# A static plan for four graph attention layers on 32 graphs: priorities re-stated, with an addition for each eighth of the work of the first three and the last three graphs

## Chip, cores and metric

The kernel runs on one core of one Trainium2 chip. The metric is the time of one execution on the device in microseconds (us); lower is better. An execution of this kernel lasts about 3440 us.

## What is computed

The input is a batch of 32 graphs (`x`, 32 x 512 nodes x 256 features, float32) and one adjacency matrix for all of them (`adj`, 512 x 512 integers). Each graph goes, independently of the others, through four residual layers. Cut to what matters:

```python
def gat(h, mask, W, a, slope):           # one graph attention head
    v = h @ W
    e = leaky_relu(v @ a_src [:, None] + v @ a_dst [None, :], slope)
    return softmax(where(mask, e, -big), axis=-1) @ v

for layer in (L0, L1, L2, L3):
    h = relu(layernorm(x))
    x = x + layer(h)
# L0: 4 heads of 64 columns, masked, elu
# L1: relu(h @ W1 + b1), a full (unmasked) attention over 512 columns + residual,
#     relu(. @ W2 + b2), a masked attention over 256 columns + residual, relu
# L2: masked attention (own node always in), elu
# L3: masked attention, relu
```

All matrix products are in float32 and run on TensorE (PE). Per graph these are the projections, the four 512 x 512 attention matrices times the values of L0, the full attention of L1, and the three masked attentions of L1, L2 and L3, besides the transposes.

## The kernel before

**Recording, then planning.** The kernel does not issue instructions as its loops run. It records *pieces*: `do(engine, ns, outs, ins, run)` (`Plan.add`) notes one piece of work with an estimated duration, its engine and the tiles that it writes and reads, and works out which pieces it must follow. A graph is recorded by `plan.begin()` and 535 pieces (the set-up has 97). The list `plan.graphs` holds 33 entries: entry 0 is the set-up (loading of weights, masks and their transposes), entries 1 to 32 are the 32 graphs.

**The order.** `Plan.order()` then plays the whole program through on a small event model: five engines (PE; VectorE, here DVE; ScalarE, ACT; GpSimd, POOL; and the DMA queue of SyncE, SP), a fixed delay from a piece to its followers (`LAG`, `SAME`, `MORE`), a port that POOL shares with those DVE pieces that read no PSUM, and a stock of buffers (`SLOTS`). Up to `DEPTH` = 5 graphs are in work at once. Whenever an engine is free, the ready piece with the lowest key is taken, where

```python
            urgency = URGENCY if b else FIRST
            ...
                p.key = (max(0, b - 1) * PERIOD - urgency[n], b, n)
```

`b` is the graph, `n` the place of the piece in its recording, and `PERIOD` = 103600 ns. So one table, `URGENCY`, holds a number of nanoseconds for each piece of a graph and serves all 32 graphs alike; a second table, `FIRST`, serves the set-up. The order that comes out fixes the order of the instructions on every engine: each instruction is tied to the one before it on its engine. Nothing is reordered at run time, an engine that has to wait holds all that stands behind it, and only semaphores decide when something starts.

**Fillers.** Where the plan sees PE without work for 400 ns or more, it puts transposes of a constant into a spare PSUM tile, `filled` (L1017), behind the piece that comes before the gap:

```python
FILL, FILL_NS, FILL_FROM = 0.6, 110, 400
...
                    before.fill = int(FILL * gap / FILL_NS) if gap >= FILL_FROM else 0
```

They compute nothing that is used. Their number tells how long a gap the plan saw: one filler for each 110 / 0.6 = 183 ns of it.

**Names that matter below.** Every graph runs the same chains:

- Layer norm: `stats`, `mv` (DVE), `rstd` (POOL, L598 and L599), `shift` (DVE, L605), `h` (ACT, L613), then transposes `tr<-h` on PE (L398) and copies into `hT`.
- A masked attention (`gat`, and `gat_heads` for L0): projection `mm<-w..,hT` (L408), scores spread over the partitions `row<-v` or `row<-st` (PE), row maxima `left`, `peak` (DVE, L654), columns `ca`, `cb` (DVE, L677, L678), a transpose `tr<-cb` (PE, L632), `turned` (ACT), a write and a broadcast read through DRAM (`line`, `rb`, L636 and L644), then four times `y` (DVE, L697), an addition on POOL (L707 or L715) and an exponential on ACT (`pt`, L708 or L722), and the product `mm<-v,pt` or `mmh<-vh,pt` (PE, L408).
- The full attention of L1: `mm<-wfc,out1T`, a maximum over all nodes that goes over PE (`row<-tmax`, L398), a few small DVE operations on `c`, one exponential on ACT (`c<-c`, L859), the transpose `tr<-c` (PE, L632), `ra` (ACT, L870), `ptf` (DVE, L877), the products `mm<-hfc,ptf`.

`transposes` and `product` record a PE piece as several matmuls. In the trace a 257-column float32 matmul of the program stands as two records, and a transpose as one.

Of the kernel before, what the change touches and what calls it, by code (L numbers as in the profile page):

```python
# [36 lines left out]
PERIOD = 103600  # L37
# [4 lines left out]


URGENCY = [
    49957, 66495, 153342, 82735, 144893, 18248, 163947, 104419, 59651, 169283, 167420, 27958, 91780, 230242,
    195004, 201919, 109150, 118275, 41409, 148351, 105924, 84158, 33663, 128315, -31046, 92771, 80073,
    -45028, 28235, 136777, -16929, 40188, 120535, 69018, 81157, 34057, 45864, 64938, 93847, 22979, 32782,
    -10095, -7685, 78515, -28222, 19420, -8026, 14562, 65514, 92596, 50809, 54059, 90452, -2420, 84889,
    -14583, 182093, 91531, 6874, 128004, -23771, -69759, 210945, 103417, 96629, 177264, 97081, 141216,
    228810, 79944, 208774, 181698, 34991, 127254, 226356, -9989, 145084, 102532, 51302, 57785, 135746,  # L50
    80518, 8900, 128919, 64999, 72213, 100118, -191301, 129287, 126778, 107678, 38434, 214310, -59056,
    21096, 128569, -77796, 31871, 74871, 45424, 52264, -8376, 19505, -47500, 133347, 67984, 70285, 186177,
    -15984, 104650, 146444, -6977, 74654, 209924, -4928, 74371, 174294, 40423, 51951, 50262, 29464, 45416,
    3988, 20540, -30268, 143961, 32626, 29520, 89804, -46895, -71848, 192873, -94019, -16097, 82357,
    -169645, 44440, 58074, 23239, 29426, 38323, 69931, 62358, 28167, 54402, 35577, -76917, -57030, -27704,
    46576, -51547, -24313, -49157, 37623, -166471, -262408, -40277, -75897, 2495, -34811, -74370, 10822,
    -15615, -38619, -14324, 87924, -14732, 53506, -26615, -76490, 65133, 111389, 71959, 93636, 216417,
    118024, 163785, 26618, -73110, 16741, 9419, -10974, -26368, 86308, 35587, -14529, 9505, -23652, 31209,
    -35827, 87676, 57894, 76693, 67541, -81967, -32754, 78132, 16981, 15839, 11266, -39752, -44185, -180983,
    -106465, -45466, -89834, -11687, 103426, 151973, 157389, 186709, 237443, 270307, 278957, 17921, 218966,  # L60
    105429, 178416, 116249, 84788, 142806, 50637, 86803, 147442, 126624, 122625, -24526, 224818, 181273,
    122134, 261099, 188560, 278444, 309233, 202098, 46668, 146708, 13559, -27972, -149859, 4547, -115510,
    38885, 107791, -163000, 38869, -279727, -120416, -64868, -65585, -103808, 25837, -296121, 16410, -66665,
    -247882, -82470, -195328, -56781, -67125, -74463, -260380, -10356, -293322, -28794, -66573, -118165,
    117861, -244495, 33153, -14981, 71927, -75326, 49632, -75897, 12372, -59742, -253914, -34455, -280537,
    60459, -56427, -20405, -76842, -84804, -76638, -87008, 6362, -96566, -92921, -140211, -40235, 9737,
    1430, 138501, -8164, -11585, -790, 92727, -18209, -59964, 33770, 120062, 48291, -69971, -116178, -43376,
    -75934, -22587, -855, -7366, 64764, -21815, -173536, -191622, -247, -89468, -141561, -5472, -71333,
    -71091, -23345, -35224, -60425, -31184, -36678, -96715, -93204, -104153, 122741, -103991, -49069,
    -52273, 103915, -129888, -87436, -90017, -84147, -248017, -153179, -142134, -195377, -246140, -94749,  # L70
    -281312, -209508, -156148, -170174, -173938, -110763, -202784, -90958, -123778, -230905, -217447,
    -158358, -191908, -181567, -150880, -166302, -173285, -145335, -192412, -213127, -112164, -79463,
    -80154, -45304, -115344, -213688, -61711, -71844, -179488, -7519, -10195, -123581, -92377, -130342,
    -156089, -168165, -158280, -78069, -97410, 20095, 52768, -118896, -100859, -22248, -140758, -98924,
    -171258, -214761, -144742, -191503, -188885, -161622, -179163, -210494, -197100, -75155, -143396,
    -114654, -120868, -88478, -67661, -85469, -105261, -231208, -147545, -195786, -143928, -132751, -203479,
    -51238, -198637, -307380, -218655, -234274, -292902, -81910, -227932, -110271, -9939, -267811, -133305,
    96531, -164689, -28167, 25068, -163586, -170683, -125323, -118603, -47000, -182274, -161878, -209482,
    -210149, -168999, -138546, -191158, -233690, -133535, -231298, -285256, -155744, -125493, -243944,
    -223209, -190911, -249846, -244877, -146750, -260327, -392277, -245282, -212678, -202761, -168108,  # L80
    -206988, -163184, -234077, -225292, -151778, -418885, -146975, -166246, -197351, -165479, -253278,
    -164022, -7427, -227404, -223194, -205947, -290945, -299944, -191474, -275233, -246375, -249699,
    -253455, -249835, -216585, -256193, -283065, -390887, -270743, -284915, -267017, -418553, -281245,
    -293102, -238408, -177593, -347600, -366149, -358476, -414408, -536943, -384769, -405112, -314429,
    -370595, -265928, -543033, -409858, -416969, -320333, -443009, -407966, -431291, -243310, -493060,
    -378266, -346645, -225670, -370270, -376164, -325328, -399421, -374586, -398079, -417234, -461239,
    -465521, -400816, -409787, -543463, -345783, -366473, -257474, -479888, -496847, -470513,
]
FIRST = [
    -31437, 25750, -1105, 144955, 89002, 275880, 128415, 204208, 154195, 226450, 96820, 179479, 7870,  # L90
    -118045, 26290, 146438, 138609, 157057, 205913, -16123, 59630, 57501, -56814, 5247, -4577, -6068,
    -45189, -27458, 74268, 87671, 62434, 55789, -15727, -51036, -133151, -170623, -122434, -106956, -88821,
    -45241, -84685, -17322, -151531, 663, -157813, -74980, -174232, -62374, -58576, 11927, -19486, -48352,
    77279, -175495, -146175, -169316, -241074, -142701, -178875, -141702, -62487, -96044, -41405, -94885,
    -228054, -41409, -191710, -235324, -125187, -188700, -74514, -165891, -142656, -170202, 6399, -96844,
    -155386, -142053, -171779, -291299, -271981, -405298, -401521, -247815, -210715, -198935, -245058,
    -90055, -125151, -183656, -54990, -77623, -143327, -261274, -244716, -325695, -246171,
]


# [43 lines left out]
class Plan:  # L144
# [57 lines left out]
    def order(self):  # L202


        for b, pieces in enumerate(self.graphs):
            urgency = URGENCY if b else FIRST
            for n, p in enumerate(pieces):
                p.waits = len(p.after)
                p.key = (max(0, b - 1) * PERIOD - urgency[n], b, n)
        free = {k: n for k, (n, _) in SLOTS.items()}  # L210
        held = [dict.fromkeys(SLOTS, 0) for _ in self.graphs]
        undone = [len(g) for g in self.graphs]
# [3 lines left out]
        events, n, oldest, admitted, done = [], 0, 0, 0, []  # L216
# [29 lines left out]
        while True:  # L246
            for e in range(len(LAG)):
# [3 lines left out]
                while ready[e]:  # L251
                    key, p = heapq.heappop(ready[e])
# [26 lines left out]
            while events and events[0][0] == now:  # L279
                _, kind, _, e, p = heapq.heappop(events)  # L280
# [789 lines left out]
```

## Time and profile before

| | |
|---|---|
| median of 3 runs | 3440.47 us (3440.38 to 3443.44) |
| the profiled execution's own time | 3439.76 us |
| its span, from first to last instruction | 3437.8 us |
| PE busy | 3397.8 us (99%), 18801 matmul records |
| DVE, ACT, POOL busy | 2629.5 us (76%), 1962.7 us (57%), 1657.1 us (48%) |
| mean granted TensorE clock | 0.998 |
| fillers (L1017) | 497, 59.5 us of PE's busy time |

Busy time counts an engine as busy while an instruction of its own is in work. A group of the profile is named by its source line, its engine, and output<-input tiles; "idle before" is the time that the engine stood still just ahead of the group's instructions. Where a row of the trace says `PEclk`, it is the share of the full TensorE clock that was granted in that stretch.

### The profile page before, as it was taken

Reading aid. Unit: us, or ns where it says so; the run is one execution under the profiler, and the core shown is the slowest. Engines: PE = TensorE matmul, PEld = TensorE weight load, DVE = VectorE, ACT = ScalarE, POOL = GpSimd, SP = SyncE. Lnnn points to the kernel's source line nnn. Section 1 sums busy time; section 2 is a strip of 40 time slices with the busy share of each in tenths; the row PEclk is TensorE's granted clock in tenths of the full one; section 3 lists DMA queues with packets and bytes.
Section 4 is the critical chain, followed back from the end, with each engine's and each line's share of the span. In section 5 each row is a group of like instructions: output and inputs, shape, how many; then the busy total and the mean of one; then the engine's idle time right before and its main releaser. Section 6 shows DMA issues by size and latency. Waiting matters only on the chain. (4 is left out here: it accounts for less than half of the span.)

```text
span 3437.8 us, 55266 instructions
## 1 busy us (share of the span) xinstructions
PE 3397.8 (99%) x18801; PEld 2861.4 (83%) x18801; DVE 2629.5 (76%) x8200; ACT 1962.7 (57%) x4109; POOL 1657.1 (48%) x2089
## 2 busy tenths in 40 slices
PE   7999999999999999999999999999999999999998
PEld 7788888888888888888888888888888888888887
DVE  8587877777777777777777877777878777777764
ACT  4555565565655565555566655556655655655543
POOL 3253554454544454545444545544544545544544
PEclk9999999999999999999999999999999999999999
DMA  3000110011110011110010110010110011110000
GB/s 111 19 29 14 35 38 31 17 38 32 35 38 26 22 38 32 35 38 26 22 38 29 37 38 26 22 37 29 38 38 21 27 32 35 38 32 16 32 19 28
DMA packets 77978, 110.51 MB, mean 32 GB/s; under 512 B 7169, under 2 KB 43521, under 8 KB 77697
## 3 DMA queue, kind: packets, MB, share of 16 engines
q1 hardware_dynamic: 77696, 106.98, 9.9%
q8 instruction: 150, 2.46, 0.3%
q14 instruction: 132, 1.07, 0.1%
HBM read 89.66 MB, written 17.30 MB: 31 GB/s over the span
## 5 line engine op out<-in xcount | busy, mean ns | idle before, releaser
L715 POOL TENSOR_TENSOR y<-y,farT_some 128x512 f32<-128x512 f32 x512 | 584.9, 1176 | 311.1 <-DVE y L697 308.3
L408 PE MATMUL mm<-v,pt 128*128 128x257 f32 x3072 | 704.1, 380 | 7.0 <-ACT pt L708 4.2
L697 DVE SCALAR_TENSOR_TENSOR y<-row,cc,rb 128x512 f32<-128x512 f32 x896 | 625.2, 742 | 73.1 <-DMA rb<-line 53.5
L408 PEld LDWEIGHTS mm<-v,pt 128*128 128x128 f32 x3072 | 575.5, 190 | 88.4 <-ACT pt L708 5.4
L722 ACT ACTIVATE pt<-y,ct 128x512 f32<-128x512 f32 x640 | 459.3, 719 | 291.2 <-POOL y L715 271.5
L408 PEld LDWEIGHTS mmh<-vh,pt 128*128 128x128 f32 x4096 | 483.3, 192 | 10.0 <-ACT pt L722 1.8
L408 PE MATMUL mmh<-vh,pt 128*128 128x65 f32 x4096 | 481.8, 272 | 1.4 <-DVE y L697 0.6
L408 PE MATMUL mm<-hfc,ptf 128*128 128x257 f32 (+1 forms) x2048 | 465.6, 381 | 0.5 <-DVE ptf L877 0.4
L408 PE MATMUL mm<-wfc,out1T 128*128 128x257 f32 x2048 | 464.4, 379 | 0.0
L408 PEld LDWEIGHTS mm<-wfc,out1T 128*128 128x128 f32 x2048 | 382.2, 189 | 53.6
L408 PEld LDWEIGHTS mm<-hfc,ptf 128*128 128x128 f32 x2048 | 380.8, 189 | 52.7 <-issue 2.0
L654 DVE CUSTOM_DVE_ANT_0 left<-row,far_nz 128x512 bf16<-128x512 f32 x640 | 413.9, 681 | 9.1 <-PE row L398 9.1
L707 POOL TENSOR_TENSOR y<-y,g 128x512 f32<-128x512 f32 x256 | 323.1, 1274 | 93.7 <-issue 42.9
L613 ACT ACTIVATE h<-xt,shift,rstd 128x256 f32<-128x256 f32 x512 | 277.5, 592 | 32.1 <-DVE shift L605 32.0
L598 POOL TENSOR_SCALAR rstd<-mv 128x4 f32<-128x4 f32 x128 | 34.3, 268 | 533.9 <-DVE mv L1014 356.0
L939 ACT ACTIVATE ez<-mm,rden 128x256 f32<-128x256 f32 x256 | 120.8, 472 | 238.6 <-DVE rden L1014 167.1
L408 PE MATMUL mm<-hT,w 128*128 128x512 f32 x512 | 233.2, 592 | 0.0
L654 DVE CUSTOM_DVE_ANT_0 left<-row,far_pos 128x512 bf16<-128x512 f32 x256 | 165.5, 685 | 86.5 <-PE row L398 86.5
L408 PE MATMUL mm<-out1T,wm 128*128 128x512 f32 x512 | 224.9, 592 | 0.0
L708 ACT ACTIVATE pt<-y 128x512 f32<-128x512 f32 x256 | 160.6, 628 | 82.7 <-POOL y L707 82.7
L1014 DVE BATCH_NORM_STATS2 stats<-xt 128x6 f32<-128x256 f32 x512 | 196.9, 414 | 5.6 <-DMA xt<-in_x_dram 5.2
L971 POOL TENSOR_TENSOR xt<-xt,rz 128x256 f32<-128x256 f32 x128 | 100.8, 797 | 199.7 <-ACT rz L970 196.3
(150 smaller groups left out, 5636.8 us busy)
## 6 DMA issues: line engine op xcount, KB each, us to landing
rb<-line SPq DMA_DIRECT2D x256, 256.0 KB
xt<-in_x_dram SPq DMA_DIRECT2D x32, 512.0 KB
out_dram<-xt SPq DMA_DIRECT2D x32, 512.0 KB
line<-turned SPq DMA_DIRECT2D x128, 2.0 KB
adj_sb<-in_adj_dram SPq DMA_DIRECT2D x1, 1024.0 KB
wfc<-in_L_gnn_W_fc_dram SPq DMA_DIRECT2D x2, 512.0 KB
a_row<-in_L_gnn_a_dram SPq DMA_DIRECT2D x3, 256.0 KB
a_row<-in_L_gnn_a_fc_dram SPq DMA_DIRECT2D x1, 512.0 KB
```

Source lines behind the costliest of these rows:

```text
L408: nc.tensor.matmul(o, lhsT=parts[k], rhs=parts[nk + k], start=(k == 0), stop=(k == nk - 1))
L598: do(POOL, 200, [rstd.all], [mv[:, :, 1]], lambda o, a: nc.gpsimd.tensor_scalar(o, a, EPS, None, ALU.add))
L613: lambda o, a, m, s: nc.scalar.activation(o, a, AF.Relu, bias=m, scale=s),
L654: return nc.vector.tensor_tensor_reduce(out=junk, in0=a, in1=far, scale=1.0, scalar=LOWEST, op0=ALU.add, op1=ALU.max, accum_out=o,)
L697: lambda o, a, c, b: nc.vector.scalar_tensor_tensor(o, a, c, b, ALU.add, ALU.max),
L707: do(POOL, 1255, [y.all], [y.all, g.all], lambda o, y, g: nc.gpsimd.tensor_tensor(o, y, g, ALU.add))
L708: do(ACT, 521, [pt[:, jt, :]], [y.all], lambda o, a: nc.scalar.activation(o, a, AF.Exp))
L715: lambda o, y, far: nc.gpsimd.tensor_tensor(o, y, far, ALU.add),
L722: lambda o, a, c: nc.scalar.activation(o, a, AF.Exp, bias=c),
L939: do(ACT, ns, [o.all], [z, scale], lambda o, a, s=scale, f=f: nc.scalar.activation(o, a, f, scale=s))
L971: do(POOL, 685, [xi], [xi, r.all], lambda o, a, b: nc.gpsimd.tensor_tensor(o, a, b, ALU.add))
L1014: made = p.run(*(r.ap() if isinstance(r, Ref) else r for r in p.args))
```

## The change

The tables of the plan change, and the key in `Plan.order()`; no operation, tile, buffer or constant of the model does. All numbers of `URGENCY` and `FIRST` are replaced. Two tables are new: `EARLY` for the first three graphs and `LAST` for the last three, each with three rows of eight numbers. A piece's place in the recording decides which of the eight it gets, and the number is added to its urgency. (`LAST`'s first row goes to the last graph, its second to the one before, and so on.)

```diff
 URGENCY = [
-    49957, 66495, 153342, 82735, 144893, 18248, 163947, 104419, 59651, 169283, 167420, 27958, 91780, 230242,
...
+    43943, 23247, 115444, 28195, 131913, 11021, 150223, 75332, 64495, 133886, 120583, -1101, 94222, 220028,
...
 FIRST = [
-    -31437, 25750, -1105, 144955, 89002, 275880, 128415, 204208, 154195, 226450, 96820, 179479, 7870,
...
+    -36661, 19893, -21726, 135503, 85633, 237464, 129132, 171706, 120477, 219412, 125455, 134502, -84836,
...
+EARLY = [
+    [127714, 124300, 140109, 1275316, 20684, 3710, 30790, 20023],
+    [21381, 1446513, 75479, -3218, 89835, 61799, 992, -5994],
+    [16582, -743, 947951, -35616, 537487, -26713, 362315, 602],
+]
+LAST = [
+    [136435, 122850, 411901, 1447410, 146100, 513359, -692128, 374735],
+    [14763, 42474, 104030, 510068, 166538, -178446, 1731034, 221293],
+    [5870, -6330, 13392, 2190, 30176, 62234, 471784, -1052314],
+]
...
+        more = {len(self.graphs) - 1 - k: row for k, row in enumerate(LAST)} | {1 + k: row for k, row in enumerate(EARLY)}
         for b, pieces in enumerate(self.graphs):
             urgency = URGENCY if b else FIRST
             for n, p in enumerate(pieces):
                 p.waits = len(p.after)
-                p.key = (max(0, b - 1) * PERIOD - urgency[n], b, n)
+                add = more[b][n * len(more[b]) // len(pieces)] if b in more else 0
+                p.key = (max(0, b - 1) * PERIOD - urgency[n] - add, b, n)
```

Below the tables the changed file's lines stand lower by 12, and below the new line of `Plan.order()` by 14 (L408 is then L422, L1017 is L1031).

## The prediction

> **What bounds the kernel now.** I read the page's busy times first, then the groups of PE with shapes kept apart, then PE's waits, then the stretches of the span, and last the order of time at the places that these point to.
>
> ```profile
> span 3437.8 us, 55266 instructions
> PE 3397.8 (99%) x18801; PEld 2861.4 (83%) x18801; DVE 2629.5 (76%) x8200; ACT 1962.7 (57%) x4109; POOL 1657.1 (48%) x2089
> L408 PE MATMUL mm<-v,pt 128*128 128x257 f32 x3072 | 704.1, 380 | 7.0 <-ACT pt L708 4.2 <-ACT pt L722 2.8
> L1017 PE MATMUL filled<-ident 128*128 128x128 f32 x497 | 59.5, 273 | 0.0
> ```
>
> PE is busy for all but 40.0 us of the span, and 59.5 us of the busy time is fillers. So PE's own work is 3397.8 - 59.5 = 3338.3 us, and 99.5 us (40.0 idle, 59.5 fillers) is all that any order could win. Is the work itself at PE's pace? In the order of time, 32 records of `mm<-v,pt` last 7.11 us where nothing disturbs them: taking off the last one's drain, 217 ns from start to start, in the middle and in the tail alike. That pace doesn't depend on the order.
>
> The Trainium skill (Perfetto Trace Analysis, Identifying the Most-Contended Engine) says that matmul busy time is a bad measure of headroom and that the busy share of LDWEIGHTS should be used instead. Here that is 83%, which would leave 17% of the span, an estimate of some 580 us, to a better order; the even 217 ns speak against it, and I go by the row.
>
> Where do the 99.5 us lie? First the fillers alone, then everything, by stretches (start and length, then busy us and instructions):
>
> ```profile
> 0.00:50.00 50.00, 12.85 (x108) 12.32 (x108) 0.93 0.57 190
> 50.00:100.00 50.00, 10.23 (x87) 9.39 (x84) 0.97 0.06 22
> 3300.00:3350.00 50.00, 8.02 (x66) 7.45 (x66) 1.00 0.05 17
> 3350.00:3400.00 50.00, 14.03 (x118) 13.16 (x118) 0.97 0.07 22
> 3400.00:3440.00 40.00, 13.26 (x114) 12.66 (x114) 0.93 0.10 34
> ```
>
> The reader sees fillers at both ends and (these rows hold 58.4 of the 59.5 us) next to none between. Of the middle, PE's rows are:
>
> ```profile
> 200.00:400.00 200.00, 199.00 (x1106) 1.00 0.08 26
> 400.00:600.00 200.00, 199.73 (x1072) 1.00 0.09 27
> 600.00:3000.00 2400.00, 2398.95 (x13180) 1.00 0.10 32
> 3000.00:3200.00 200.00, 200.00 (x1104) 1.00 0.10 30
> ```
>
> PE stands still for 2.3 us in these 3000. The middle can hardly get better; the ends can.
>
> **How the order moves.** Both programs hold the same 11136 PE instructions of the program besides fillers. The fillers are 497 before and 381 after. By place: start 194 -> 217 (the two long groups, 68 and 61, become 74 and 62, and 15 new ones come about 250 to 300 us in); end 303 -> 164. At the end the groups 27, 12, 23, 66, 77 become many groups of 2 to 15 and, last, 22 and 48: the chains of the last graphs, which ran one behind the other with nothing beside them, now lie beside each other, and the very last product is for two graphs (32 records by 2) rather than one.
>
> **What a filler stands for.** A filler is not the gap; the gap is filler plus the wait behind it. Two of the long ones before:
>
> ```profile
> 3376.38 7.37 PE L1017 MATMUL filled<-ident 128*128 128x128 f32 x66
> 3386.55 15.84 PE L408 MATMUL mm<-v,pt 128*128 128x257 f32 x64 [2.81 <-ACT pt L722]
> 3413.68 8.57 PE L1017 MATMUL filled<-ident 128*128 128x128 f32 x77
> ```
>
> 66 fillers stand for 7.4 + 2.8 = 10.2 us without work. For all of the start: fillers 12.85 + 10.23 + 0.38 = 23.5 us, idle time 9.8 us (19.7 us idle in the first 200 us, less the 9.9 us before PE's first instruction), so 33.3 us for 194 fillers, 0.171 us each. For all of the end: fillers 36.0 us, idle 12.6 us (PE's waits there, without the 5.4 us after its last matmul), so 48.6 us for 303, 0.160 us each.
>
> - Start: 23 more at 0.171 us: **+3.9 us**.
> - End: 139 fewer at 0.160 us: **-22.3 us**.
> - Together **-18.4 us**. Bounds: only the fillers' own PE time goes and the waits behind them stay, 116 x 59.5 / 497 = -13.9 us; or the whole gap that the plan saw goes, 116 x 183 ns = -21.3 us. I stay with the traced ratio, which is from the same kind of place.
>
> The set-up's first PE instruction waits for the same mask (9.9 us, DVE `m_nz`), with the same loads of `x` and `adj` ahead of it: nothing. After the last matmul the same steps follow for one graph (5.4 us): nothing. The moved loads of weights on SP come after `adj` as before, and the first group that needs them is behind the same 9 fillers: nothing; if one came late, the price is its landing, a few us at most.
>
> **The clock.** After the waits of 3.79, 4.15 and 2.81 us the granted clock falls: 0.56 in 40 to 46 us, 0.79 in 82 to 90 us, 0.61 in 3386 to 3390 us. Each fall costs 1.7 to 1.8 us: 16 `row<-ca` took 3.65 us against 1.91 us of the same shape at full clock; 64 `mm<-v,pt` took 15.84 us against 14.06 us. The first two waits stand in the new order too, the third has no group of 66 behind it any more, but the last group of 48 may bring one: 0 to -1.8 us, I take **-0.9 us**.
>
> The Trainium skill (TensorE: Matmul & The Clock Gate, Part 1) puts the fall to half rate after an idle window of about 3.4 us. By that the 2.81 us wait would have cost nothing and the third term would be 0; and it speaks against an order with more, shorter groups, as each leaves part of its gap bare. The row with 0.61 decides for me.
>
> **The middle.** Here the whole order is new, and PE waits for nothing: what costs is any chain that now comes late. I measured the cover of each chain, the PE work (at the traced paces) that stands between the PE instruction that starts it and the one that needs its end. Both orders run a cycle that repeats from about the sixth graph. Where the new one is thinner (us before -> after): `tr<-cb` to the first `mmh` 18.4 -> 14.0; last `mm<-w2x` to `tr<-cb` 13.7 -> 7.1; last `mm<-v,pt` to `tr<-h` 9.9 -> 8.0; `row<-tmax` to `tr<-c` 4.0 -> 2.7. The first needs 8.5 us to its first `pt` in the trace (1514.74 to 1523.3), the second 4.8 us in the bare tail (3371.0 to 3375.8), the third 8.1 us in the tail (3395.3 to 3403.4) with a POOL addition of 0.8 us and an ACT step of 0.45 us of other chains in its way, which the new order doesn't put there, so some 6.9 us. The fourth is the tight one:
>
> ```profile
> 1514.63 0.27 PE L398 MATMUL row<-ident,tmax 128*128 128x128 f32 x1
> 1514.94 0.29 DVE L848 TENSOR_REDUCE tmax<-row 128x1 f32<-128x128 f32 x1
> 1517.01 0.42 DVE L961 SCALAR_TENSOR_TENSOR ez<-ez,rz 128x256 f32<-128x256 f32 x1 [0.91 <-ACT ez L959]
> 1518.29 0.20 ACT L859 ACTIVATE c<-c 128x16 f32<-128x16 f32 x1
> 1518.76 0.27 PE L632 MATMUL tr<-ident,c 128*4 128x128 f32 x1
> ```
>
> Before, the chain takes 3.9 us, with a 0.91 us DVE wait for ACT and three `h` on ACT in its way. In the new order the `c` operations follow each other on DVE with one small operation between them; adding up the starts of its own links in this stretch (0.31, 0.33, six DVE steps of 0.1 to 0.2, 0.33, 0.26) gives 2.4 us against 2.8 us from the start of `row<-tmax`. But on ACT four `h`, two `ez`/`rz` and an exponential now stand ahead of `c`, and these wait for `shift`, which stands behind three `left` (0.61 us each) on DVE. I reckon a wait of 0 to 0.3 us in each of the 23 graphs of the cycle: 0 to 7 us (and at best the 2.3 us that stand idle now are won), and take 0.1 us, **+2.3 us**. PE's order is fixed, so everything behind `tr<-c` waits too, and nothing gives it back.
>
> **Sum.** -18.4 - 0.9 + 2.3 = -17.0 us. The profiled execution's own 3439.76 us becomes 3422.8; the median, 0.7 us above it, becomes 3423.5 us.
>
> **The rivals.** About 0.2%, 6.9 us, is what a measurement of this kernel can tell from no change: below 3433.6 us is faster, above 3447.4 us slower.
>
> *The cycle stalls (slower).* The chain from `row<-tmax` keeps the 3.9 us that it took before, and the fourth `h` ahead of it on ACT (0.52 us) comes on top: 4.4 us against 2.8 us is a wait of 1.6 us in each of 23 graphs, +36.8 us: 3440.5 - 18.4 - 0.9 + 36.8 = 3458.0. It decides once each graph stalls by over 1.14 us ((18.4 + 0.9 + 6.9) / 23); from 0.54 us on the result is within 0.2%. For it: the four `h` ahead of `c`, and a plan's delays are fixed numbers. Against it: most of the 3.9 us was other work between the chain's own links, and that is moved out of it.
>
> *The fillers go, the waits stay (faster by less).* The gaps at the end close only where fillers were; -13.9 + 3.5 (0.15 us by 23): 3430. For it: waits of 1 to 3 us stood behind the long groups. Against: fewer long groups are left.
>
> *The plan's gaps are not the chip's (no change).* Were the gaps at the end only the plan's view, the time would stay near 3440. Against it: 0.160 and 0.171 us of real time per filler, beside the plan's 0.183.
>
> *More comes back.* The whole 21.3 us, and all three falls of the clock (5.3 us): 3413.9.
>
> **How the numbers follow.** My forecast with its small variants (3414 to 3430) gets 0.74; fillers only, or a little stall (3430 to 3437), 0.10; no change or a stall of about 0.5 us per graph, 0.08; the stalled cycle, 0.08. Faster: 0.74 and most of the second case, 0.82; within 0.2%: 0.10; slower: 0.08. The range goes from 3414, the sum of the favourable bounds, to 3437, where fillers alone go and 0.45 us stalls per graph: -13.9 + 10.4.
>
> **What would show it.** Right: PE idle and fillers together near 80 us, fillers 45 to 47 us, PE's work still 3338 us, middle stretches idle by a few us only, the tail's long group of about 48 followed by a wait of 1 to 3 us. Wrong: `tr<-c` or `tr<-h` with waits that come 20 times or more, or a PE middle of less than 2990 in 3000 us.

## The result, and the profile after

The changed kernel takes 3436.05 us (median of 14 runs, 3431.00 to 3441.39), the kernel before in the same sessions 3440.43 us (median of 14 runs, 3434.74 to 3447.01). The ratio is 0.9985, with a 95% interval from 0.9977 to 0.9993. So it is faster by 0.15% by the ratio, or 4.4 us by the medians: outside its own noise, but under the 0.2% that the prediction called a change, and far from the 17.0 us that it forecast. It lies in the stated range (3414 to 3437), by 1 us. One execution of e7 below, of 12493.85 us at a mean clock of 0.476, is left out of its figures. The profiled execution of after took 3439.92 us (span 3438.2), against 3439.76 us (span 3437.8) before: in these two the whole gain is missing, which makes them good to compare.

First the lines that answer to those shown of before: the page, and the groups of PE.

```profile
span 3438.2 us, 55054 instructions
PE 3400.9 (99%) x18685; PEld 2852.8 (83%) x18685; DVE 2678.3 (78%) x8200; ACT 1965.3 (57%) x4109; POOL 1640.6 (48%) x2089
L422 PE MATMUL mm<-v,pt 128*128 128x257 f32 x3072 | 704.5, 380 | 2.1 <-ACT pt L722 2.0
L1031 PE MATMUL filled<-ident 128*128 128x128 f32 x381 | 47.8, 275 | 0.0
```

Idle time and fillers fell as forecast in kind: 99.5 us before, 37.3 + 47.8 = 85.1 us after. But PE's *own* work, which cannot have changed (the same matmuls), rose from 3338.3 to 3400.9 - 47.8 = 3353.1 us. 14.8 us of "busy" time are new, and they eat the 14.4 us.

Where? The transpose `row<-tmax` stands once in each graph. From its start in the sixth graph to its start in the thirtieth are 24 rounds of the cycle. These rows give its first and last start in that part, for before and after:

```profile
L398 PE MATMUL row<-ident,tmax x25: 272/272/273, 580.7 to 3072.8; 128*128 128x128 f32 x25
L412 PE MATMUL row<-ident,tmax x25: 272/273/273, 591.0 to 3095.1; 128*128 128x128 f32 x25
```

So the start is 10.3 us longer, the middle 12.0 us (2492.1 -> 2504.1), and the end, up to PE's last matmul at 3432.4 us in both, 22.3 us shorter (359.6 -> 337.3). PE's busy time in these three stretches, before and then after:

```profile
0.00:581.00 581.00, 560.05 (x3181) 0.99 0.12 38
581.00:3073.00 2492.00, 2490.95 (x13681) 1.00 0.10 31
3073.00:3433.00 360.00, 346.83 (x1943) 1.00 0.08 27
```

```profile
0.00:591.00 591.00, 568.89 (x3202) 0.98 0.12 37
591.00:3095.00 2504.00, 2501.10 (x13686) 1.00 0.10 31
3095.00:3433.00 338.00, 330.92 (x1801) 1.00 0.10 28
```

The second row of each is the surprise: of the 12 us that the middle lost, PE's idle time shows 1.9 (1.05 -> 2.90); the other 10 are booked as busy. Stretches of the start and of the end, after (the fillers alone: start and length, then busy us and count of PE and PEld, the clock):

```profile
50.00:100.00 50.00, 11.49 (x96) 10.57 (x94) 0.83 0.05 15
3300.00:3350.00 50.00, 3.22 (x22) 2.62 (x22) 1.00 0.09 25
3350.00:3400.00 50.00, 7.80 (x58) 6.73 (x58) 1.00 0.14 39
3400.00:3440.00 40.00, 9.50 (x81) 9.00 (x81) 0.94 0.15 42
```

The end has 164 fillers of 21.0 us where it had 303 of 36.0 us (three of the 164 stand ahead of these rows), and its idle time fell by 6.1 us more. That is 21.1 of the 22.3 us. The rest fits the fall of the clock at 3386.9 us, worth some 1.7 us, which before had and this execution has not. The first row shows a clock of 0.83 where before had 0.97.

**Where the hidden waits are.** Going by starts rather than by busy time, the median round of the cycle is 103.75 us before and 104.15 us after, which makes some 9.5 us in 24 rounds. The other 2.5 us of the middle lie in a few longer rounds (up to 105.59 us), in three of which PE shows a wait of 0.76 to 0.85 us for DVE. Of the 0.4 us of the median round, 0.27 lie in the projection `mm<-w2x`. PE's weight loads (PEld) show it, in before and after:

```profile
L408 PEld LDWEIGHTS mm<-w2x,hT 128*128 128x128 f32 x512 | 92.5, 191 | 23.5 <-issue 14.3
L422 PEld LDWEIGHTS mm<-w2x,hT 128*128 128x128 f32 x512 | 90.7, 191 | 31.4 <-ACT hT L1028 10.1 <-issue 7.3 <-DVE top L688 5.5
```

10.1 us of weight loads that wait for an ACT copy `hT` are new. The first eight `mm<-w2x` of one round, before, and then the same place in one round of after, in order of time:

```profile
1559.36 1.91 PE L408 MATMUL mm<-w2x,hT 128*128 128x258 f32 x8
```

```profile
1571.73 0.72 ACT L736 ACTIVATE pt<-y,ct 128x512 f32<-128x512 f32 x1 [0.39 <-POOL y L729]
1571.94 2.18 PE L422 MATMUL mm<-w2x,hT 128*128 128x258 f32 x8
1572.36 0.56 ACT L1028 COPY hT<-tr 128x512 f32<-128x512 f32 x1
1572.98 0.73 PEld L422 LDWEIGHTS mm<-w2x,hT 128*128 128x128 f32 x4 [0.41 <-ACT hT L1028]
```

Eight `mm<-w2x` at 217 ns last 1.91 us with the drain; in after they last 2.18 us, and no gap is shown. A matmul record is 380 ns long while the next may start after 217 ns, so up to 163 ns of standing still at each place look like work. What is waited for is no data: the copy that ends at 1572.92 is of another graph's `hT`. The program's allocation shows that the second product of `mm<-w2x` is put into the PSUM bank that this copy reads from: of the 7 banks that the plan deals out, five are in use at this place, and two are just being given back. The copy stands behind an exponential on ACT.

**The clock at the start.** In this execution the granted clock was at half for 6.8 us at 38.8, for 13.7 us at 59.2 and for 3.4 us at 90.0; before it was 6.8 us at 38.4 and 3.4 us at 82.8. The extra 13.7 us at half clock are worth at most 6.9 us. With 3.3 us of fillers and 1.2 us of idle time more, that is up to 11.4 us for the 10.3 us of the start; the mix of work in this stretch is not quite the same in both orders, and the 1.1 us were not followed up.

### The profile page after: what moved, and what is told of

It is laid out like the page before. It is cut to its first block, busy times and chain, and to the rows that moved or that the text cites. A ratio compares the mean times of both kernels' runs of the same rounds, so it can differ in the third digit from the quotient of the medians.

```text
span 3438.2 us, 55054 instructions
## 1 busy us (share of the span) xinstructions
PE 3400.9 (99%) x18685; PEld 2852.8 (83%) x18685; DVE 2678.3 (78%) x8200; ACT 1965.3 (57%) x4109; POOL 1640.6 (48%) x2089
## 3 DMA queue, kind: packets, MB, share of 16 engines
q1 hardware_dynamic: 77696, 106.98, 10.3%
## 5 line engine op out<-in xcount | busy, mean ns | idle before, releaser
L422 PE MATMUL mm<-v,pt 128*128 128x257 f32 x3072 | 704.5, 380 | 2.1 <-ACT pt L722 2.0
L422 PEld LDWEIGHTS mm<-v,pt 128*128 128x128 f32 x3072 | 573.6, 190 | 85.7 <-ACT pt L722 4.0
L422 PEld LDWEIGHTS mmh<-vh,pt 128*128 128x128 f32 x4096 | 489.2, 193 | 11.7 <-issue 1.9
L422 PE MATMUL mmh<-vh,pt 128*128 128x65 f32 x4096 | 485.3, 274 | 1.1 <-ACT pt L736 0.7
L422 PE MATMUL mm<-hfc,ptf 128*128 128x257 f32 (+1 forms) x2048 | 474.1, 381 | 1.2 <-DVE ptf L891 0.9
L422 PE MATMUL mm<-wfc,out1T 128*128 128x257 f32 x2048 | 471.1, 379 | 0.0
L422 PEld LDWEIGHTS mm<-wfc,out1T 128*128 128x128 f32 x2048 | 382.2, 189 | 53.4
L422 PEld LDWEIGHTS mm<-hfc,ptf 128*128 128x128 f32 x2048 | 379.1, 190 | 52.8 <-POOL y L729 2.2
L974 POOL TENSOR_TENSOR rz<-rz,res 128x256 f32<-128x256 f32 x128 | 93.7, 733 | 316.2 <-ACT rz L953 310.7
L422 PE MATMUL mm<-hT,w 128*128 128x512 f32 x512 | 230.7, 593 | 0.0
L422 PE MATMUL mm<-out1T,wm 128*128 128x512 f32 x512 | 225.2, 592 | 0.0
L422 PEld LDWEIGHTS mm<-out1T,wm 128*128 128x128 f32 x512 | 95.0, 190 | 107.0 <-issue 99.7
```

The lines of the kernel that those rows point to most:

```text
L422: nc.tensor.matmul(o, lhsT=parts[k], rhs=parts[nk + k], start=(k == 0), stop=(k == nk - 1))
L974: do(POOL, 685, [r], [r, res[:, it, :]], lambda o, a, b: nc.gpsimd.tensor_tensor(o, a, b, ALU.add))
```

## The experiments

Each comparison is with the kernel before, run in the same session. "Start", "middle" and "end" are the three stretches above, from the profiled execution.

**e1: the changed kernel once more.** Only a comment differs.

> The changed kernel itself, as the yardstick of the three beside it. In the profiled executions so far the start (to the sixth graph's row<-tmax) is 10.3 us longer than before, the 24 graphs after it 12.0 us longer, the end 22.3 us shorter. Theory A (two separate losses: a clock that falls to half for 13.7 us at the start in some executions, and a wait for a PSUM buffer in each graph of the cycle): the time follows the mean granted clock of each execution, 3.4 us for each 0.001, and is 3431 to 3440 us; the cycle is 104.1 us in every execution. Theory B (one loss: the new order makes PE slower as such): the cycle itself would vary with the clock.

Median 3436.51 us (3431.65 to 3441.07), ratio 0.9987 (0.9978 to 0.9996). The profiled execution had a clock of 0.999 and a span of 3431.5 us: start 583.6, middle 2504.3, end 337.8 us. The middle and the end are those of the first profile to 0.5 us; the start is 7.4 us shorter. Two rows of each execution tell why, the products of the heads at the start (in order of time), and PE in the stretch from 60 to 73 us. After, then e1:

```profile
56.59 11.54 PE L422 MATMUL mmh<-vh,pt 128*128 128x65 f32 x64 [0.69 <-ACT pt L736]
60.00:73.00 13.00, 13.00 (x64) 0.50 0.01 2
```

```profile
55.08 7.36 PE L422 MATMUL mmh<-vh,pt 128*128 128x65 f32 x64 [0.69 <-ACT pt L736]
60.00:73.00 13.00, 13.00 (x120) 1.00 0.01 2
```

The same 64 matmuls behind the same wait of 0.69 us took 11.54 us at half clock and 7.36 us at full. PE is busy for all 13.00 us in both. So these 7.4 us of the start are the clock's, and they differ between executions of one program; the middle does not. Theory A holds, B falls.

**e2: one ACT pair exchanged.** In the changed kernel's `Plan.order()`:

```diff
+        act = [p for p in done if p.engine == ACT]
+        for a, b in zip(act, act[1:]):
+            if (a.key[2], b.key[2]) == (138, 17) and b.graph == a.graph + 1:
+                done.remove(a)
+                done.insert(done.index(b) + 1, a)
         return done
```

> In each graph of the cycle one ACT pair is exchanged: the exponential pt (recorded place 138) that stands right ahead of the copy hT (place 17 of the next graph) goes right behind it; all else, fillers included, is as in the changed kernel. Theory A: the projection mm<-w2x takes the PSUM bank that this copy gives back, so its wait (0.41 us on PEld in the trace, 0.27 us per graph from start to start) goes: cycle 104.15 -> 103.9 us, mm<-w2x busy 134.8 -> about 129 us, time 6 us less than the changed kernel beside it. Rival (the pace of PE in the new order, for example from more changes between kinds of matmul): the cycle stays 104.1 and the time stays.

Median 3434.03 us, ratio 0.9978 (0.9969 to 0.9986). The middle is 2499.0 us (5.1 less than after), the median round 103.94 us. In the group of the weight loads the wait for the copy is cut by half (10.1 us after):

```profile
L427 PEld LDWEIGHTS mm<-w2x,hT 128*128 128x128 f32 x512 | 90.7, 190 | 26.6 <-issue 7.3 <-DVE top L693 5.5 <-ACT hT L1033 5.5
```

In one round, in order of time, the copy now starts at 1570.51, as soon as its transposes are there:

```profile
1570.31 1.98 PE L427 MATMUL mm<-w2x,hT 128*128 128x258 f32 x8
1570.51 0.59 ACT L1033 COPY hT<-tr 128x512 f32<-128x512 f32 x1 [0.80 <-PE tr L417]
```

The 2.18 us became 1.98. Two operations of ACT in each graph are worth 0.21 us of each round. The rival, a slower PE in the new order, falls for this half of the median round's loss. The other 0.19 us stay; by starts they are spread over `mm<-hfc`, `mm<-w2x`, `mm<-w3x` and `tr<-ef` with under 0.1 us each, and were not followed up. The median of all runs fell by 2.5 us only, against 5.1 in the profile; in the next pair it is clearer.

**e3 and e4: fuller gaps.**

```diff
-FILL, FILL_NS, FILL_FROM = 0.6, 110, 400
+FILL, FILL_NS, FILL_FROM = 0.85, 110, 400
```

e3 has this edit alone, e4 this and the one of e2.

> FILL is 0.85 in place of 0.6, so 381 fillers become about 545 and cover most of each gap; the order is that of the changed kernel. Clock theory: the falls of the granted clock at the start (6.8, 13.7 and 3.4 us at 0.5 in the profiled execution, 23.9 us, some 12 us of PE time lost of which part was idle) go or get shorter; mean clock 0.999 or more, 5 us less than the changed kernel beside it and a smaller spread. Rival (the start is longer because of its waits alone): no gain, or 1 to 3 us more where a filler ends later than the gap.

> Both edits together. If both theories hold: 11 us less than the changed kernel, about 3425 us, and 0.4% below the kernel before. If only the exchange works: as e2. If neither: as the changed kernel.

e3: 3432.58 us, ratio 0.9978 (0.9969 to 0.9986); the profiled execution has no fall of the clock before PE's last matmul, and a start of 583.1 us. That is 3.9 us less than e1 by the medians, somewhat less than expected. e4: 3427.36 us, ratio 0.9963 (0.9950 to 0.9975): another 5.2 us by the medians, nearly the 6 us that the exchange was to give. Against e1 the medians fall by 2.5 us (e2), 3.9 us (e3) and 9.2 us (e4): neither gain eats the other, and the middle falls from 2503.3 us (e3) to 2497.4 (e4). The two losses are separate.

**e5: the same fill with the order before.** `FILL` is 0.85 in the kernel before.

> The kernel before with FILL 0.85 in place of 0.6 (497 fillers become 705), its order untouched. Clock theory: the three falls of its profiled execution (6.8, 3.4 and 3.4 us at half clock) go, and the time falls by about 5 us to 3435, spread smaller; so most of what FILL 0.85 brings has nothing to do with the change, and the two orders at equal clock differ by some 3432.6 - 3435 = -2 us only. Rival (the change made the clock worse, and only its order profits): no gain here.

3436.47 us against 3442.66 us beside it, ratio 0.9985 (0.9976 to 0.9993): 6.2 us less. In the profiled execution one fall of the clock is left at the start (3.4 us at 82.0). The fuller gaps help both orders, and are no merit of the change. With them the two orders stand at 0.9978 and 0.9985 of the kernel before, with intervals that overlap.

**e6 and e7: the additions taken out.**

```diff
-        more = {len(self.graphs) - 1 - k: row for k, row in enumerate(LAST)} | {1 + k: row for k, row in enumerate(EARLY)}
+        more = {} | {1 + k: row for k, row in enumerate(EARLY)}
```

for e6, and `add = 0` for e7.

> The changed kernel with LAST taken out (EARLY and the new tables stay): 217 fillers at the start as in the changed kernel, 327 at the end in place of 164. Theory (one filler stands for 0.160 us of the end): start and cycle as in the changed kernel (104.1 us), end 337 + 163 x 0.160 = 363 us, time some 26 us above the changed kernel, 3462, slower than before by 0.6%. Rival (the chip is more forgiving than the plan at the end): under 10 us above the changed kernel.

> The changed kernel with neither EARLY nor LAST, the new URGENCY and FIRST alone: 1053 fillers (381 in the changed kernel), and now also in the middle, some 22 in each three graphs. Theory (the additions at the start decide into which cycle the plan settles; one filler stands for 0.165 us wherever it is): 672 more fillers are +111 us, 3547 us, with cycles that are no longer alike from graph to graph but repeat every three. Rival (an addition for the first graphs reaches only the first graphs): a middle of 104.1 us cycles and fillers at the ends alone.

e6: 3468.68 us, ratio 1.0076 (1.0062 to 1.0090). Start 590.8 and middle 2503.4 us are the changed kernel's; the end is 367.9 us in place of 337.3: 30.6 us for 163 fillers, 0.19 us each, a little over the forecast. Fillers and idle time make up 25.9 us of it, 0.159 us each; in the rest, this execution has two falls of the clock near its end (10.2 us at half, from 3404.2 and 3452.0 us) that after has not. `LAST` alone carries the gain at the end, and with the new tables but without it the end is worse than before's 359.6 us.

e7: 3638.01 us (median of three executions), ratio 1.0561 (1.0542 to 1.0580). The middle is 2623 us, a mean round 109.3 us. An addition for the first three graphs reaches all the others: it decides which repeating order the plan settles into. The direction was forecast, the size was not: some 200 us above e1 for 672 fillers, 0.30 us each rather than 0.165. Between the two profiled executions (214 us apart) fillers and idle time make up 158 us, 0.24 us for each filler; the other 56 us are PE's own work, which takes longer. In this execution of e7 the clock fell to half ten times between 640 and 2970 us, mostly for 6.8 us, behind gaps that come back every third graph; its mean is 0.986.

**e8: no fillers at all.** `FILL` is 0 in the changed kernel.

> The changed kernel with FILL 0: no fillers, the order untouched. Clock theory: PE stands still for the whole 85 us, each gap of more than about 3 us is followed by a fall to half clock (about 1.75 us each, the two long ones at the start and some eight at the end), mean clock 0.99, +10 to +20 us against the changed kernel. Rival (fillers only fill the record): within 3 us of it.

3445.31 us, ratio 1.0009 (1.0000 to 1.0018), so 0.22% or 7.6 us above the changed kernel by the ratios, just under the forecast range. The clock was at half for 13.7, 20.5 and 13.7 us within the first 95 us. Start and end are 590.8 and 340.4 us (e1: 583.6 and 337.8), though idle time and fillers together fell from 80.1 us in e1 to 68.2: it is PE's own work that takes longer. What the fillers buy here is clock.

**e9 and e10: the cycle before with an end of its own.** If the end's gain is real and the middle's loss a separate thing, then the tables of before with additions for the last three graphs alone should keep both. `URGENCY` and `FIRST` are those before, `EARLY` is gone, and `LAST` was found by a random search in the plan's own model:

```diff
+LAST = [
+    [11863, 53409, 63943, 7589717, 3323038, 987900, 18131, -33167],
+    [12126, -157392, 551313, 1415199, 514259, 1969446, -63868, -132820],
+    [10232, 8303, -7483, 12206702, -92300, -776774, -6093694, -5121875],
+]
```

> The tables URGENCY and FIRST of the kernel before, with no EARLY, and a LAST of its own for the last three graphs (24 numbers, searched for the fewest gaps in the plan). Start and cycle keep the order before; fillers 497 -> 379, almost the 381 of the changed kernel, 118 fewer at the end. Theory (the end's gain is real and worth 0.160 us a filler; the changed kernel lost it to its cycle and start, which are not made by the shorter end): start 580 us, 24 cycles in 2492 us, end 359.6 - 18.9 = 341 us, so 19 us below the kernel before, 0.9945. Rival (the gaps that the plan closes come back on the chip whatever the cycle is, as in the changed kernel): 4 us below the kernel before, 0.9985.

> The same with FILL 0.85 (546 fillers). If the gains of e9 and of the fuller gaps add up: 19 + 6 = 25 us below the kernel before, about 3416 us, 0.993, the fastest of all. If the rival of e9 holds: 10 us below.

e9: 3428.27 us, ratio 0.9967 (0.9955 to 0.9979); e10: 3424.42 us, ratio 0.9953 (0.9940 to 0.9965), 15.7 us below before (25 were expected) and the fastest kernel of all by its median (its interval overlaps that of e4). e9 has 379 fillers, the changed kernel 381, and yet it is 6 us faster by the ratios, 8 us by the medians: the number of fillers does not tell the time. The rival (4 us) falls, but the forecast of 19 was too much as well. In the profiled execution of e9 the start is 581.9 us, middle and end together 2839.8 us against 2851.7 before. PE's busy time in that stretch, then the fillers alone, before and then e9:

```profile
580.70:3432.40 2851.70, 2838.05 (x15624) 1.00 0.10 31
580.70:3432.40 2851.70, 36.02 (x303) 1.00 0.10 31
```

```profile
581.90:3421.70 2839.80, 2828.27 (x15506) 1.00 0.10 31
581.90:3421.70 2839.80, 23.95 (x185) 1.00 0.10 31
```

Idle time and fillers fell by 14.2 us (13.65 + 36.02 to 11.53 + 23.95), so 2.3 us are lost again where the idle column does not show it. The clock does not explain them: each of the two executions has one fall for 3.4 us there (at 3386.9 us before, at 3148.7 us in e9). They were not traced.

## Why the prediction was wrong

*The end* (-22.3 us): measured -22.3. The ratio of real time to filler, taken from the same place of the trace before, held: 21.1 us for 139 fillers, 0.152 us each, and 0.159 in e6. That the sums agree to the tenth is luck, as the measured one holds the fall of the clock that I had booked under the clock. `LAST` is what makes the gain (e6).

*The start* (+3.9 us): 4.5 us of fillers and idle time in the profile; right.

*The clock* (0 to -1.8 us, taken as -0.9): this term failed. I counted which waits would be left and gave each the fall that it had before, 1.7 to 1.8 us. But a fall does not belong to a wait. The same program had 23.9 us at half clock in the start in one execution and 6.8 us in another (after, e1), and a fall at the narrow products of the heads lasted 13.7 us where those priced lasted 3.4 or 6.8. Before had 13.6 us at half clock up to PE's last matmul, so the term is at most -3.4 us in e1 and +5.2 us in after: it varies from run to run. e3 and e5 show that fuller gaps take most of it away, in either order.

*The middle* (+2.3 us): measured +12.0, the largest miss. The step that failed is the list of covers. I measured chains by the work between their ends, named four that had become thinner, and priced `row<-tmax` to `tr<-c` as the tight one; its wait came to 0.3 us in total. The wait that did come was one that no cover by data can show: for a PSUM bank, freed by an ACT copy that the plan had put behind an exponential. By starts it is 0.27 us in each median round, 6.5 us in 24; e2 took back 5.1 us of the 12.0. Of the rest, 2.5 us lie in a few longer rounds, and the cause of the other 3 us or so, spread over several groups, stays open. And the sign that I gave for it, PE's idle time in the middle, was blind to it: I took "the even 217 ns" as a property of PE and "busy" as work, though a record lasts 380 ns. The Trainium skill (Perfetto Trace Analysis, Identifying the Most-Contended Engine), whose rule I set aside, was half right here: the busy share of matmuls did hide 10 us, and waits of the weight loads pointed to most of them. But their 83% was no headroom of 17% for any order tried: e10, the fastest, takes 3424.42 us at 84%.

*Sum*: fillers and idle time -21.1 at the end and +4.5 at the start, the middle +12.0, and a clock of -3.4 to +5.2 us: -8.0 to +0.6 us. The measured -4.4 lies in it. My rival of the stalled cycle had the mechanism of the loss (a repeated small wait, in each of some 24 graphs) and the size at which it would reach no change (0.54 us a graph; measured 0.5, clock apart), but in another place and at a chance of 0.08.

## What to carry to other kernels

An order that an offline model has searched out is best on that model; ask what the model does not hold before its gaps are booked as time. Here these were a bank that came free later on the chip than by the model's estimated durations (the model does count banks), and a clock. 10 us of the middle's loss stood in no idle column: where records overlap, compare starts from one round to the next, and read the waits of the weight loads. Such a wait alone is no loss yet, since loads run beside matmuls; the starts decide. A gain at the ends of a long run is easily paid back by a few tenths of a microsecond in each round of its middle, so keep a middle that is at its floor and tune the ends on top of it (e9, e10).

## What the hardware showed unexpectedly

Once the clock had fallen to half, 13 us of PE work without a gap did not raise it: from 59.2 to 72.9 us it stayed at 0.50, all of it 65-column and 128-column float32 matmuls, where the other two falls of the start of that execution ended after 6.8 and 3.4 us. The Trainium skill (TensorE: Matmul & The Clock Gate, Part 1) says that one busy window of about 3.4 us is enough; this execution disagrees. And falls came without a long wait: ahead of this one PE had stood still for 1.75 us (the row below) and for 0.69 us (at 56.59, shown with e1) only.

```profile
53.55 1.16 PE L422 MATMUL mm<-w0x,hT 128*128 128x264 f32 x4 [1.75 <-DVE y L711]
```
